# Graph network of four layers: the last two row chunks of layer 3 by gathered neighbour lists instead of dense products

## The chip, the cores and the metric

The kernel runs on one core of a Trainium2 chip. Times are device microseconds (us) of one execution. Three timed runs of the kernel before gave 2332.58, 2321.81 and 2318.35 us, so the median is 2321.81 us. The profile and the trace come from another execution, under the profiler, which took 2299.72 us; its span, from the first instruction to the last, is 2297.7 us.

The engines are called PE (TensorE, matrix products), PEld (its weight loads), DVE (VectorE), ACT (ScalarE), POOL (GpSimd) and SP (SyncE). A transfer (DMA) is issued by SP, ACT or POOL and carried by 16 DMA engines.

## The reference

A graph of 2708 nodes has a 0/1 adjacency matrix `adj` (about 0.6% ones, symmetric) and 512 features a node. Four layers follow each other, each with a residual and a layer norm:

```python
x = layernorm(x + relu((D(A + I)D x + x) W0 + b0))     # layer 0
x = layernorm(x + (D' A D' x) W1.T + b1)               # layer 1
x = layernorm(x + gat(gat(x)))                         # layer 2: two attention layers
#   gat(x): Wh, Ws = split(x W2); a = softmax(Wh Ws.T) * A; leaky_relu(a Wh + x)
x = layernorm(x + A x W3 + b3)                         # layer 3 (8 heads side by side: one 512x512 W3)
```

All of it is float32; the change is about layer 3, `A x W3`.

## The kernel before

**Tiles.** The nodes are cut into 22 blocks of 128 (`NB`; the last has 20 nodes). Output nodes are also cut into six chunks `CH`: chunks 0 to 3 have 512 nodes (four blocks each), chunk 4 has 384 (blocks 16 to 18), chunk 5 has 276 (blocks 19 to 21). The blocks that are summed over are cut into six groups `GROUPS`: four of four blocks, then two of three.

**Dense products (layers 0, 1 and 3).** `multiply` (line 894) forms the transposed sum `acc[d] = sum over j of x[j][:, d].T @ m[j]` for the four quarters `d` of the features, where `m[j]` is the 128 x 512 piece of the adjacency matrix. `prepare` (808) has ACT cast `m` from a byte mask, which SP loads (`load_bytes`, 798), one group ahead of the products. x is held as a high and a low part, so a (chunk, block) pair costs eight products[...]. `evict` (969) copies `acc` to `ht`, and `project` (986) multiplies by the weights in float32[...]: 16 products for a chunk of four blocks. `residual` (1015) fetches the rows `xres` of x for the skip connection, `biased` (1021) adds the bias to them on DVE, `combine` (1027) adds the projection, and `finish` (1058) normalizes and stores.

**Attention (layer 2).** After softmax, scores times neighbours are not formed densely. For each node block, layer 1 made lists of the nodes that have a neighbour in the block (`index`, 1200, into `givers`): four lists of 128 for the whole block and two for each quarter of it, twelve in all; the block of 20 has three. Attention writes a table `pairs` to DRAM, whose row for a node holds the node's features next to its weights. `fetch` (1677) has POOL gather the 128 rows of a list into one of eleven buffers `g`, and `weigh` (1732) multiplies weights by features on PE, in float32. While this goes on, `early` (605) already runs layer 3's products for chunks 0, 1 and 2 (`TWO = 3`) over the first 16 blocks, and puts the sums aside as `begun`. `Attention.normalize` (1796) ends a chunk of the last attention layer and stores its rows as `saved[2]`, from where layer 3 reads its residuals.

**Order.** Each engine works through its instructions in the order in which the code issues them (`Ordered`, 54). SP and POOL issue transfers in that order too, and a wait at one holds all behind it. Eight completion semaphores serve the transfers of SP; a transfer first waits for the one eight before it. PSUM has two halves of four banks. A chunk's four `acc`, its four projections and the next chunk's `acc` in the same half take the same four banks in turn: the next `acc` waits until DVE's `combine` has read the projection before it.

**The last stage.** After attention, layer 3 does groups 4 and 5 of chunks 0 and 1, then of chunk 2, then chunks 3, 4 and 5 whole. The projection of a chunk comes one step after its products (`step`, 1120, and `ends`, 1180).

Of the kernel before, what the change touches and what calls it, by code (L numbers as in the profile page):

```python
# [19 lines left out]
P = 128  # L20
N = 2708
# [20 lines left out]
FAR = 4096  # L42
PAGES, WIDES = 82, 11
TWO = 3
LN_EPS = 1e-5
DEG_EPS = 1e-8
SLOPE = 0.01
# [40 lines left out]
class Kernel:  # L88


    def __init__(self, ctx, tc, x_in, x_t, adj, adj_t, w0, b0, w1, b1, w2, w2_t, w3, b3, out):
        self.tc, self.nc = tc, tc.nc
        nc = self.nc
        self.ctx = ctx
        self.x_in, self.x_t, self.adj, self.adj_t, self.out = x_in, x_t, adj, adj_t, out
        self.w0, self.b0, self.w1, self.b1, self.w2 = w0, b0, w1, b1, w2
        self.w2_t, self.w3, self.b3 = w2_t, w3, b3
        const = ctx.enter_context(tc.tile_pool(name="const", bufs=1))
        self.small = ctx.enter_context(tc.tile_pool(name="small", bufs=4))
        scratch = ctx.enter_context(tc.tile_pool(name="scratch", bufs=1, space=DRAM))  # L100
        tile_ = lambda name, shape, dt: const.tile(shape, dt, tag=name, name=name)
        self.ident = tile_("ident", [P, P], FP)
        self.ones = tile_("ones", [P, P], FP)
        self.ones_b = tile_("ones_b", [P, P], BF)

        self.rdeg = tile_("rdeg", [P, NB], FP)
        self.dis = tile_("dis", [P, NB], FP)
        self.nbad = len(CH) * NB
        self.bad = tile_("bad", [P, self.nbad + NB], FP)


        self.feeds = tile_("feeds", [P, NB, QUARTERS, NB], BF)
        self.givers = tile_("givers", [P, NB, LISTS], I32)

        self.base = tile_("base", [P, QUARTERS], FP)
        self.upto = tile_("upto", [P, P], BF)
        self.node = tile_("node", [P, 1], FP)
        self.block = tile_("block", [P, NB], BF)
        self.since = tile_("since", [P, P], BF)
        self.saved = [  # L120
            [scratch.tile([P, D], FP, tag=f"x{s}_{i}", name=f"x{s}_{i}") for i in range(NB)]
            for s in range(3)
        ]
        self.between = [
            scratch.tile([P, D], FP, tag=f"y_{i}", name=f"y_{i}") for i in range(NB)
        ]

        self.masks = [
            scratch.tile([P, NB, w], U8, tag=f"mask{k}", name=f"mask{k}")
            for k, (_, w) in enumerate(CH)  # L130
        ]

        self.turned = [
            [
                scratch.tile([P, DC, w], FP, tag=f"t{s}_{k}", name=f"t{s}_{k}")
                for k, (_, w) in enumerate(CH)
            ]
            for s in range(2)
        ]
# [345 lines left out]
    return rest + [[q * ONLY + t for q in range(QUARTERS)] for t in range(ONLY)]  # L485


def cost(columns):

    return 4 * columns / 2400  # L490
# [25 lines left out]
class Fast:  # L516
# [18 lines left out]
    def run(self):  # L535
        kernel, nc = self.k, self.nc
        with ExitStack() as ctx:
            pool = lambda name, bufs, **kw: ctx.enter_context(
                self.tc.tile_pool(name=name, bufs=bufs, reuse_waits="tile", **kw)
            )  # L540
            self.pages, self.wides = pool("pages", PAGES), pool("wides", WIDES)
            self.small, self.lists = pool("small_f", 4), pool("lists", 1)
            self.banks = [pool(f"banks{h}", 4, space=PSUM) for h in range(2)]
            given = [kernel.x_in[bass.ts(i, P), :] for i in range(NB)]
            l0 = Layer(0, given, kernel.w0, kernel.b0)
            l1 = Layer(1, kernel.saved[0], kernel.w1, kernel.b1)
            l3 = Layer(3, kernel.saved[2], kernel.w3, kernel.b3)
            self.attention = attention = Attention(self)
            self.jobs, self.due, self.other, self.beats = [], None, 1, 0
            run = Run(l0, l1)  # L550
            for t in range(len(run.seq)):
                self.step(run, t)
            attention.project(attention.layers[0], 0)
            for g in range(3):
                self.ends(run, g)
                if g == 1:
                    attention.project(attention.layers[0], 1)


            run = Run(l3)  # L560
            run.seq = [(l3, k, g) for k in range(TWO) for g in range(4)]
            run.seq += [(l3, k, g) for g in (4, 5) for k in range(2)]
            run.seq += [(l3, k, g) for k in range(2, TWO) for g in (4, 5)]
            run.seq += [(l3, k, g) for k in range(TWO, len(CH)) for g in range(len(GROUPS))]
            attention.run(self.early(run))
            for j in range(*GROUPS[5]):
                l3.rows[j] = attention.made[j]
            for t in range(4 * TWO, len(run.seq)):
                self.step(run, t)

            ly, k = run.before
            parts = self.project(ly, k)
            for some in (parts[:-1], parts[-1:]):
                made = []
                for i, n, ps in some:
                    made.append((i, n, self.combine(ly, k, len(made), i, n, ps)))
                self.finish(ly, k, made)
# [230 lines left out]
    def prepare(self, ly, k, g, between=None, late=False):  # L808


        nc, (c0, cw) = self.nc, CH[k]
        ats = ly.done.pop(("at", k, g), None)
        if ats is None:
            return
        ms = []
        for j, at in zip(range(*GROUPS[g]), ats):
            if k == 0:
                self.halve(ly, j)
            m = self.page(f"m{ly.number}_{k}_{j}", FR)
            nc.scalar.copy(m[:, :cw], at[:, :cw])  # L820
            ms.append(m)
            if between:
                between()
                between = None
        ly.done["m", k, g] = ms
        if ly.number == 0:
            self.examining = self.examine(ly, k, g, ats)
            if k == 0 or g > 0:
                self.checked()
            else:  # L830
                next(self.examining)
        if ly.number == 1:
            at = ly.done.pop(("bytes", k, g))
            if late:
                return lambda: self.note(k, g, at)
            self.note(k, g, at)

    def note(self, k, g, at):

# [54 lines left out]
    def multiply(self, ly, k, g, only=None, ds=range(DC)):  # L894
# [3 lines left out]
        starts, stops = ((0, 16), (15, NB - 2)) if two else ((0,), (NB - 2,))  # L898
        if blocks[0] in starts and 0 in ds:

            half = 0 if two and blocks[0] == 0 else k
            ly.acc[k] = [self.bank(half, f"acc{ly.number}_{k}_{d}") for d in range(DC)]
        ms = ly.done["m", k, g]
        if blocks[-1] == NB - 1:
# [16 lines left out]
        for d, j in todo:  # L921
            for x, first in ((ly.hi, True), (ly.lo, False)):
                nc.tensor.matmul(
                    ly.acc[k][d][:, :cw],
                    x[j][:, bass.ts(d, P)],
                    ms[j - GROUPS[g][0]][:, :cw],
                    start=(j in starts and first),
                    stop=(j in stops and not first),
                )

    def degrees(self, ly, k):
        nc, cw = self.nc, CH[k][1]
# [53 lines left out]
    def project(self, ly, k):  # L986
# [4 lines left out]
        for i, lo, n in sorted(blocks_of(k), key=lambda b: b[2] > QW):  # L991
            if n <= QW:
                ps = self.few(
                    k,
                    f"mm{ly.number}_{i}",
                    n,
                    D,
# [2 lines left out]
                )  # L1000
                parts.append((i, n, ps))
                continue
            ps = self.bank(k, f"mm{ly.number}_{i}")
            for c in range(DC):
                nc.tensor.matmul(
                    ps[:n],
# [8 lines left out]
    def residual(self, ly, k):  # L1015
        for i, _, _ in blocks_of(k):
            t = self.page(f"xres{ly.number}_{i}")
            self.nc.gpsimd.dma_start(t, ly.source[i])
            ly.done["xres", i] = t

    def biased(self, ly, k):
# [98 lines left out]
    def step(self, run, t):  # L1120
# [5 lines left out]
            self.attention.blank()  # L1126
        if ly.number == 1 and k == len(CH) - 1 and g in (2, 3, 4):
            self.attention.begin(g - 2)
        if ly.number == 0 and g == len(GROUPS) - 1:
            self.multiply(ly, k, g, ds=range(2))  # L1130
            ends = self.degree_ends(ly, k)
            next(ends)
            self.multiply(ly, k, g, ds=range(2, DC))
        else:
            self.multiply(ly, k, g)
        if g == len(GROUPS) - 1 and k in ly.begun:
            self.evict(ly, k)
        wide = CH[k][1] == BANK
# [1 line left out]
            self.work("PE")  # L1140
        if run.before:
            self.ends(run, run.phase)
            run.phase += 1
            if run.phase in ((3, 4, 5) if wide else (4,)):
                self.work("DVE")
# [239 lines left out]
class Attention:  # L1385
# [29 lines left out]
    def blank(self):  # L1415
# [3 lines left out]
        for pairs in (p for ly in self.pairs for p in ly):  # L1419
            self.nc.sync.dma_start(  # L1420
                pairs[N:, : 2 * PAIR + D].rearrange("j (r d) -> j r d", d=D),
                t[:n, :].unsqueeze(1).to_broadcast([n, (2 * PAIR + D) // D, D]),
            )

    def begin(self, step):

# [369 lines left out]
    def normalize(self, ch):  # L1796
# [4 lines left out]
        def rest():  # L1801
            for _ in work:
                pass
            for (i, _, _), (r, _) in zip(ch.blocks, ch.ends):
                self.nc.sync.dma_start(self.k.saved[2][i], r)
                self.made[i] = r

        self.later(4, rest)


    def run(self, next_layer):
# [108 lines left out]
            yield from self.project_steps(ly, k)  # L1920


@with_exitstack
def kernel(
    ctx: ExitStack,
# [60 lines left out]
```

## Time and profile before

| What | Value |
|---|---|
| Median of the timed runs | 2321.81 us (2318.35 to 2332.58) |
| The profiled execution, its span | 2299.72 us, 2297.7 us |
| PE busy | 2269.4 us, 99% of the span |
| DVE, ACT, POOL busy | 1391.5, 675.5, 705.4 us |
| Moved by DMA | 486.34 MB, 212 GB/s on average |
| Attention's last list product on PE | starts at 2087.05 us |
| Last layer 3 product over the mask | ends at about 2277 us |

A window line of the profile gives, for a stretch of the span, each engine's busy time with its count of instructions, then the granted PE clock (1.00 is full speed), the share of the DMA engines that was busy, and GB/s. A line of the chain gives start, duration, and the engine, line and tile of the work that set the end. Almost all instructions go through a helper that keeps the order, so they carry its line, L71, and are told apart by their tiles. Each float32 product stands in the records as two.

### The profile page before, as it was taken

What the parts mean: (1) busy time and instruction counts of PE and PEld (TensorE: products, weight loads), DVE (VectorE), ACT (ScalarE), POOL (GpSimd) and SP (SyncE); (2) the same over time, 40 slices, a digit from 0 to 9 for tenths busy, and PEclk for the clock granted to TensorE, in tenths of its full rate; (3) what the DMA queues carried; (4) which work ended last, traced back from release to release, by engine and by line L of the source; (5) the groups of instructions that cost most, each with busy time, mean ns of one, the idle gap of its engine ahead of it and who ended that gap; (6) DMA issues with size and microseconds to landing.
All of it is one profiled execution on the core that took longest, in us unless ns stands there. A gap on an engine that the chain in (4) does not pass through costs nothing.

```text
span 2297.7 us, 25903 instructions
## 1 busy us (share of the span) xinstructions
PE 2269.4 (99%) x8525; PEld 1289.0 (56%) x8525; DVE 1391.5 (61%) x2803; ACT 675.5 (29%) x1354; POOL 705.4 (31%) x822
## 2 busy tenths in 40 slices
PE   9999999999999999999999999999999999899997
PEld 6776876777644444443555444444443555466685
DVE  6777787786553537748667511238769788525523
ACT  7444452322111123223322200113223334342211
POOL 3433431111000001635557540001635467442000
PEclk9999999999999999999999999999999999999999
DMA  9966752223547415858789997405868799963311
GB/s 351 286 188 184 199 168 81 76 81 104 208 184 267 144 25 184 303 191 297 254 311 360 349 412 284 183 8 179 303 218 286 254 322 339 334 217 120 116 51 43
DMA packets 260929, 486.34 MB, mean 212 GB/s; under 512 B 40238, under 2 KB 126950, under 8 KB 260784
## 3 DMA queue, kind: packets, MB, share of 16 engines
q1 hardware_dynamic: 192128, 269.63, 33.6%
q0 software_dynamic: 68656, 214.96, 28.0%
q8 instruction: 69, 1.13, 0.2%
q14 instruction: 76, 0.62, 0.1%
HBM read 307.55 MB, written 176.92 MB: 211 GB/s over the span
## 4 chain that ended last, share of the span: by engine, by line
PE 86%; DMA 6%; DVE 4%; ACT 1%; issue 1%; POOL 1%; SPq 0%; ACTq 0%; POOLq 0%; DVEq 0%
PE sp L71 33%; PE acc L71 30%; PE mm L71 8%; PE z L71 6%; PE wst L71 6%; DMA x<-x 2%; DMA x<-in_x 1%; DMA at<-in_adj_t 1%; DMA g<-pairs,givers 1%; PE mix L71 1%; DMA pairs<-s 1%; POOL xt L71 1%; PE list L71 1%; ACT m L71 1%; PE tr_x2t L71 0%
## 5 line engine op out<-in xcount | busy, mean ns | idle before, releaser
L71 PE MATMUL sp<-xs,wst_sb 128*128 128x512 f32 (+3 forms) x2112 | 798.3, 544 | 0.0
L71 POOL DMA_INDIRECT g<-pairs,givers x510 | 524.2, 1028 | 872.9 <-issue 338.9
L71 PEld LDWEIGHTS sp<-xs,wst_sb 128*128 128x128 f32 (+1 forms) x2112 | 379.7, 186 | 408.4 <-issue 324.8
L71 PE MATMUL acc<-m,xh 128*128 128x512 f32 (+4 forms) x1584 | 566.8, 379 | 6.6 <-ACT m L71 5.1
L71 PE MATMUL acc<-m,xl 128*128 128x512 f32 (+4 forms) x1584 | 549.6, 365 | 2.0 <-DVE xl L71 1.8
L71 PEld LDWEIGHTS acc<-m,xh 128*128 128x128 f32 (+1 forms) x1584 | 288.0, 188 | 70.9 <-issue 21.3
L71 PEld LDWEIGHTS acc<-m,xl 128*128 128x128 f32 (+1 forms) x1584 | 288.3, 188 | 46.3 <-issue 5.3
L71 PE MATMUL acc<-g 128*32 128x512 f32 (+1 forms) x1020 | 264.8, 606 | 4.6 <-DMA g<-pairs,givers 4.0
L71 ACT COPY s<-sp 128x512 f32<-128x512 f32 (+2 forms) x252 | 132.7, 528 | 396.8 <-PE sp L71 395.1
L71 ACT ACTIVATE s<-s 128x512 f32<-128x512 f32 (+3 forms) x264 | 151.6, 580 | 319.8 <-DVE s L71 319.5
L71 DVE TENSOR_TENSOR top<-top,s 128x512 f32<-128x512 f32 (+2 forms) x240 | 149.1, 621 | 156.1 <-ACT s L71 154.5
L71 PE MATMUL mm<-w,ht 128*128 128x512 f32 (+1 forms) x528 | 223.7, 593 | 0.0
L71 ACT CAST m<-at 128x512 fp32r<-128x512 uint8 (+5 forms) x396 | 199.2, 567 | 62.3 <-DMA at<-mask 19.7
L71 DVE TENSOR_TENSOR s<-s,shift 128x512 f32<-128x512 f32 (+3 forms) x264 | 162.7, 620 | 36.2 <-ACT shift L71 36.2
L71 DVE TENSOR_TENSOR s<-s,a 128x512 f32<-128x512 f32 (+3 forms) x264 | 165.8, 628 | 13.6 <-DMA a<-mask 4.5
L71 DVE TENSOR_TENSOR sum<-sum,s 128x512 f32<-128x512 f32 (+4 forms) x252 | 156.5, 621 | 15.4 <-ACT s L71 15.4
L71 PEld LDWEIGHTS mm<-w,ht 128*128 128x128 f32 (+1 forms) x528 | 95.8, 186 | 117.0 <-issue 112.2
L71 PEld LDWEIGHTS acc<-g 128*32 128x32 f32 (+1 forms) x1020 | 74.6, 134 | 148.0 <-issue 116.5
L71 PE MATMUL z<-w,xt 128*128 128x512 f32 (+1 forms) x352 | 151.0, 596 | 0.0
L71 PE MATMUL wst<-xt,mixed 128*128 128x512 f32 (+2 forms) x384 | 150.5, 544 | 0.0
L71 POOL DMA_DIRECT2D x<-o x44 | 26.0, 597 | 329.7 <-DVE o L71 325.4
L71 PEld LDWEIGHTS wst<-xt,mixed 128*128 128x128 f32 x384 | 72.0, 190 | 71.1 <-issue 58.8
(168 smaller groups left out, 1476.7 us busy)
## 6 DMA issues: line engine op xcount, KB each, us to landing
pairs<-z_sb SPq DMA_DIRECT2D x84, 768.0 KB
pairs<-s SPq DMA_DIRECT2D x168, 256.0 KB
at<-in_adj_t SPq DMA_DIRECT2D x84, 256.0 KB
xres<-x POOLq DMA_DIRECT2D x44, 256.0 KB, 4.6
x<-o POOLq DMA_DIRECT2D x43, 256.0 KB, 3.4
pairs<-s SPq DMA_DIRECT2D x84, 128.0 KB
x<-x SPq DMA_DIRECT2D x37, 256.0 KB
at<-mask SPq DMA_DIRECT2D x32, 256.0 KB
```

Of the source, the lines that this page charges most:

```text
L71: ins = call(*args, **kw)
```

## The change

Chunks 4 and 5 of layer 3 (blocks 16 to 21) are computed as attention does it, from a table `sided` in DRAM. A row of it holds a node's adjacency weights and its features, three copies of the features with weights between them (2196 numbers a row).

1. The weights of chunks 4 and 5 are written in layer 1: after each cast of `m`, `give` has ACT issue two transfers of it to the table, 88 in all.
2. The features of blocks 0 to 11 are written by SP from `Attention.normalize`, three copies in one transfer (`aside`), twelve transfers of 768 KB.
3. The features of blocks 12 to 21 are written after attention, by SP, from `saved[2]`: ten transfers of 768 KB from DRAM to DRAM.
4. `Listed` then fetches 63 lists with POOL, multiplies, turns the sum with PE's transposes, projects, and ends the blocks in pairs. Its products are put between those of chunk 3.
5. Order of the last stage: groups 4 and 5 of chunks 0 and 1, chunk 3 whole with the lists beside it, then groups 4 and 5 of chunk 2. `half_of` gives the PSUM halves for that order.
6. `residual` of layer 3 issues its loads from SP instead of POOL.
7. `blank` writes zeros to the table's unused rows.

```diff
+DENSE = 4
+LISTED = CH[DENSE][0] // P
+SIDED = D + 2 * P
...
             run.seq += [(l3, k, g) for g in (4, 5) for k in range(2)]
+            run.seq += [(l3, k, g) for k in range(TWO, DENSE) for g in range(len(GROUPS))]
             run.seq += [(l3, k, g) for k in range(2, TWO) for g in (4, 5)]
-            run.seq += [(l3, k, g) for k in range(TWO, len(CH)) for g in range(len(GROUPS))]
             attention.run(self.early(run))
             for j in range(*GROUPS[5]):
                 l3.rows[j] = attention.made[j]
+            for i in range(CH[TWO][0] // P, NB):
+                attention.aside(i, kernel.saved[2][i])
+            self.listed = Listed(self, l3)
             for t in range(4 * TWO, len(run.seq)):
+                if t == len(run.seq) - 2:
+                    self.listed.end_all()
                 self.step(run, t)
...
             m = self.page(f"m{ly.number}_{k}_{j}", FR)
             nc.scalar.copy(m[:, :cw], at[:, :cw])
             ms.append(m)
+            if ly.number == 1 and k >= DENSE:
+                self.give(k, j, m)
...
+    def give(self, k, j, m):
+        n, lo, cw = rows_of(j), 0, CH[k][1]
+        while lo < cw:
+            i = (CH[k][0] + lo) // P - LISTED
+            w = min(P if i % 2 == 0 else 2 * P, cw - lo)
+            at = i // 2 * SIDED + i % 2 * (D + P)
+            self.nc.scalar.dma_start(
+                self.k.sided[j * P : j * P + n, at : at + w], m.bitcast(FP)[:n, lo : lo + w]
+            )
+            lo += w
...
+    def half_of(self, ly, k):
+        return k if ly.number < 3 else (0, 1, 1, 0)[k]
...
             t = self.page(f"xres{ly.number}_{i}")
-            self.nc.gpsimd.dma_start(t, ly.source[i])
+            (self.nc.sync if ly.number == 3 else self.nc.gpsimd).dma_start(t, ly.source[i])
...
                 self.nc.sync.dma_start(self.k.saved[2][i], r)
+                if ch.k < TWO:
+                    self.aside(i, r)
...
+    def aside(self, i, rows):
+        to, copies = self.k.sided[i * P : (i + 1) * P, P:], (NB - LISTED) // 2
+        self.nc.sync.dma_start(
+            bass.AP(to.tensor, to.offset, [to.ap[0], (SIDED, copies), (1, D)]),
+            rows.unsqueeze(1).to_broadcast([P, copies, D]),
+        )
...
+class Listed:
+    AHEAD = WIDES - 1
...
+    def fetch_ahead(self):
+        nc = self.nc
+        while self.to_fetch and len(self.fetched) < self.AHEAD:
+            i, t = self.to_fetch.pop(0)
+            if ("xres", i) not in self.ly.done:
+                x = self.ly.done["xres", i] = self.f.page(f"xres3_{i}")
+                nc.sync.dma_start(x, self.ly.source[i])
+            g = self.f.wide(f"g3_{i}_{t}")
...
+            nc.gpsimd.indirect_dma_start(
+                out=g[:, :width],
+                out_offset=None,
+                in_=self.k.sided[:, :],
+                in_offset=bass.IndirectOffsetOnAxis(ap=self.k.givers[:, i, t : t + 1], axis=0),
+                element_offset=(i - LISTED) // 2 * SIDED + first,
+            )
...
+    def weigh(self, wait=False):
...
+        for h, g in enumerate(gs):
+            lo, rows = (h * QW, QW) if side else (0, n)
+            e, z = (D + lo, 0) if odd else (0, P - lo)
+            nc.tensor.matmul(
+                self.acc[lo : lo + rows],
+                g[:, e : e + rows],
+                g[:, z : z + D],
+                start=first,
+                stop=last,
+            )
...
+    def turn(self, i, n, acc):
...
+        r = f.page(f"sum3_{i}")
+        nc.vector.tensor_copy(r[:n], acc[:n])
+
+        def turn():
+            ps = f.bank(self.half, f"tr3_{i}", (P, DC, P))
+            for c in range(DC):
+                nc.tensor.transpose(
+                    ps[:, c, :n], r[:n, bass.ts(c, P)], self.k.ident[:n, :n]
+                )
+            t = f.page(f"turned3_{i}", FP, (P, DC, P))
+            nc.scalar.copy(t[:, :, :n], ps[:, :, :n])
+            x = self.ly.done["xres", i]
+            nc.vector.tensor_add(x[:n], x[:n], self.ly.bt[:n])
+            self.advance(0.45)
+            self.later(2, lambda: self.project(i, n, t))
+
+        self.later(2, turn)
```

## The prediction

> **What bounds the kernel now.** I read the busy table first, then windows of the last 400 us, then the chain in order of time, then the timelines of PE, DVE, POOL and SP around the change.
>
> ```profile
> PE 2269.4 (99%) x8525; PEld 1289.0 (56%) x8525; DVE 1391.5 (61%) x2803; ACT 675.5 (29%) x1354; POOL 705.4 (31%) x822
> ...
> 1900.00:1950.00 50.00, 47.29 (x199) 28.34 (x198) 45.58 (x92) 20.21 (x46) 36.94 (x35) 1.00 1.01 357
> 1950.00:2000.00 50.00, 42.66 (x150) 22.29 (x148) 26.23 (x62) 17.75 (x33) 26.96 (x30) 0.95 0.94 351
> 2000.00:2090.00 90.00, 88.53 (x381) 59.15 (x380) 33.17 (x76) 32.27 (x64) 40.62 (x45) 0.99 0.68 216
> 2090.00:2276.00 186.00, 186.00 (x822) 134.75 (x821) 73.19 (x160) 42.98 (x100) 9.64 (x18) 1.00 0.22 75
> ```
>
> PE has no idle time in the last stage (186 of 186 us): there every product removed counts, and every wait added counts too. From 1900 to 2000 it is another matter: the DMA engines are full (1.01 and 0.94) and PE idles 10 us.
>
> ```profile
> 1921.51 11.97 DMA x<-x
> 1933.50 8.83 DMA pairs<-s
> ...
> 1956.06 10.54 DMA x<-x
> 1966.67 11.98 DMA x<-x
> ...
> 2110.89 13.73 PE mm L71 x32
> ...
> 2206.62 13.73 PE mm L71 x32
> 2220.35 28.38 PE acc L71 x175
> 2248.73 10.30 PE mm L71 x24
> 2259.03 18.06 PE acc L71 x143
> ```
>
> The chain shows the prices of the last stage, and that around 1920 to 1980 loads of 256 KB stand 10 to 12 us behind other transfers. Next, when the residual rows of chunk 0 are there and who needs them (POOL, SP, then DVE):
>
> ```profile
> 2080.07 2.24 POOL L71 DMA_DIRECT2D xres<-x  x4
> ...
> 2094.17 1.31 SPq L71 DMA_DIRECT2D x<-r  x3
> ...
> 2107.03 2.48 DVE L71 TENSOR_TENSOR xres<-xres,bias 128x512 f32<-128x512 f32 x4
> 2109.44 2.47 DVE L71 TENSOR_TENSOR ht<-acc,begun 128x512 f32<-128x512 f32 x4
> ```
>
> POOL asks for them at 2080, so DVE adds the bias at 2107 without waiting and goes on to chunk 1's `ht`. SP stores the last rows of attention at 2094.
>
> **What the Trainium skill says.** "DMA: Bandwidth & Descriptors", Latency and other measured facts: copies between two DRAM tensors run at 207 to 214 GB/s in each direction. The trace of before has no such copy; it has loads and stores mixed at 412 GB/s in its best slice, so a copy that both reads and writes DRAM at half of that fits. Same page, Issuing engines are not separate DMA queues: all issuers share 16 engines. The trace agrees, with loads 12 us late at share 1.01. Same page, Anatomy of one DMA: about 2 us fixed per transfer; quiet stores here land after 2.7 us at the least. "TensorE: Matmul & The Clock Gate", Part 1: after some 3.4 us of idleness PE runs at half rate for as long. The trace agrees: after an idle 4.08 us before 1997.27, four pairs of products take 1.04 us each instead of 0.45.
>
> **The change, part by part**, against the profiled execution (span 2297.7, execution 2299.72 us).
>
> *Products removed.* Of chunk 5, groups 1 to 5 are the last 18.06 us; its group 0 (32 products at 0.128) is 4.1. The 28.38 us piece is chunk 4's groups 1 to 5 and that 4.1, so 24.3; its group 0 (32 at 0.174) is 5.6. Together **-52.0**. Six projections remain: 18 us in either kernel.
>
> *Products added.* In attention's part of the chain a pair of whole lists takes 1.72 us and four quarter lists 0.99. A block is 2 x 1.72 + 2 x 0.99 = 5.4, five blocks 27.1, the block of 20 (three lists at 0.86) 2.6: **+29.7**. The turns: 24 transposes at 0.13 (10.9 us for 84) give **+2.7**. Net on PE: -19.6.
>
> *End of the lists.* For block 20 nothing covers DVE's copy of the sum (0.69) and ACT's copy of the turn (0.6), with handovers **+1.8**. The other blocks have a quarter chunk's products (1.8 us) and list products between. *Tail:* the last chunk has four blocks instead of three. Behind its `ht` DVE must finish chunk 3's last two blocks, its normalization, and four bias adds, before the first sum. I find the last DVE sum some 2.9 us after PE's last product; before it was 0.8. **+2.3**.
>
> *Fetches.* 63 at 1.26 us (0.95 and 0.30 between) are 79 us of POOL, beside 77 us of PE work from the first list to the last, with ten fetched ahead. If they start 11 us before the first list, they cost nothing; without that cover each us late is a us lost. They start when the table is whole, see below.
>
> *Writes of weights.* Each cast of `m` in layer 1's chunks 4 and 5 is followed on ACT by two issues that wait for it. The trace has no issue on ACT; SP's cost 0.32 to 0.46 us. So a block costs ACT 0.5 + 0.1 + 0.7 = 1.3 us, and PE needs 1.4 (chunk 4) or 1.0 us (chunk 5) for its products, with projections and turns between (562 to 596 us for chunk 5's 22 blocks, against 29 us of ACT and its own copies). Queued behind are the later casts, on which PE waits. Lower bound 0, upper 6 (22 x 0.3). I take **+2**: the last two groups come late.
>
> *Feature copies in attention.* Four of 768 KB a chunk are 3.1 MB, 8.6 us at 360 GB/s. Chunk 0's come at 1692 and chunk 1's at 1791; there POOL has just begun to fetch, and PE weighs only at 1714 and 1814, so I cost these at nothing (without that slack, up to 8 each). Chunk 2's come at 1888. Until 1900 about 4 us of DMA time are free, then none until 1985; on SP chunk 4's `pairs`, the masks and the x loads of layer 3 are behind them. **+5**, bounds 0 and 12.
>
> *Late copies and the residuals behind them.* This is the large term. SP issues the ten copies from 2095.5, 7.86 MB. At 214 GB/s that is 36.7 us, with 1.5 to start: over at 2133.7. In SP's queue the residual loads now come after them: two for the lists, then blocks 0 to 3. Block 3's is the sixth of 256 KB; 4.6 us at 340 GB/s and 2 to land give 2140.3. DVE meets `biased` for chunk 0 at 2107 and waits there. Behind it are chunk 1's `ht` and chunk 0's `combine`, and chunk 3's four `acc` need the banks that `combine` frees. PE would be through chunk 3's group 0 at 2090.7 + 20.2 (groups 4 and 5) + 13.7 (projection) + 7.3 = 2131.9. Now DVE ends the last bias add at 2140.9, `ht` at 2143.4, the first sum at 2144.1 (quarter d0 may start), the second at 2145.7, then statistics and four bias adds for chunk 1, the third sum at 2149.7, the fourth at 2151.3. PE leaves group 0 at 2153.1: 21.2 us late. The fetches start at about 2136 and share the engines with these loads, some 2 us more. **+23**. Bounds: at 390 GB/s (a store-like rate, 20 us) it is +4; at 150 GB/s (52 us) +38. As PE stands so long, the fetches get their ten ahead and cost nothing more.
>
> *Blank rows* are four small issues in layer 0, beside 250 GB/s of loads: 0.
>
> Sum: -19.6 + 1.8 + 2.3 + 2 + 5 + 23 = +14.5, so 2314.2 for the profiled execution's 2299.72. The median of the timed runs is 22 us (1.0%) higher than this execution; I scale: 2321.81 x 1.0063 = **2336 us**, +0.6%.
>
> **Rivals.**
> *Fast copies.* If DRAM to DRAM runs as stores do (340 GB/s, 23 us), the residual term is 23 - 13.6 = +9, the sum about 0: 2322. For it: 412 GB/s in a slice. Against it: every byte both leaves and enters DRAM.
> *The saving shows.* If the residuals do not wait for the copies (loads overtaking them in the rings), 23 falls to 0 and the sum is -8.5: 2313; with the attention and ACT terms at nothing too, 2306. Against it: 12 us behind other transfers in the chain above.
> *Slow copies, on the other side.* Pieces of 2 KB at 150 GB/s take 52 us. DVE gets past `biased` only at 2156, the term is +38 and the sum +30: 2352, slower by 1.3%. It becomes slower by over 1% when the copies need more than 46 us. For it: the copies go in pieces of 2 KB, three from the same row. Against it: stores of the same pieces ran at 390 GB/s between 1350 and 1400.
>
> **How the numbers follow.** A measurement of this kernel can tell about 1% from no change. Forecast (copies near 200 GB/s) 0.50, mostly between 2325 and 2346; fast copies 0.17; the saving shows 0.10; slow copies or a longer stall 0.23. Faster by over 1% (below 2298.6) needs more than all the PE time that is saved: 0.04. Slower by over 1% (above 2345): most of the slow case and the top of the forecast, 0.30. Within 1%: 0.66. The range leaves out the best of the saving and the worst of the slow case: 2308 to 2357.
>
> **What would show it.** PE idle in the last stage after chunk 0's projection, with DVE in `biased` waiting for `xres` until about 2140; `sided` copies on SP from 2095 and first fetches about 2136; then no waits on lists. More PE idle time than 10 us between 1900 and 2010. ACT's share higher in 500 to 600 us with PE short of `m` by 2 us. PE's busy time down by about 20 us. I am wrong if the copies are over by 2115, if DVE does not stand at the bias, or if PE waits on lists.

## The result and the profile after

The changed kernel takes 2352.98 us (median, 2344.19 to 2358.07); the kernel before, timed beside it, 2320.12 us. The ratio is 1.0122 with a 95% interval of 1.0089 to 1.0154: slower by 1.2%. On another chip, where the kernel before takes 2303.5 us, it is 1.0096 (1.0074 to 1.0119). The time lies in the range given, 17 us above the forecast. How it comes about is less well forecast than that suggests.

The first lines are the changed kernel's own page: engine shares, then the transfer queue of ACT, which is new.

```profile
PE 2279.2 (97%) x8323; PEld 1260.4 (53%) x8323; DVE 1393.7 (59%) x2812; ACT 662.1 (28%) x1313; POOL 753.5 (32%) x863
...
q10 hardware_dynamic: 12216, 7.15, 1.0%
```

PE has 202 products fewer, but its busy time is not lower (2279.2 us, before 2269.4) and its share falls from 99% to 97%: it stands idle more, and more of its products run at half clock (the mean granted clock is 0.984, before 0.997).

The first two traces are not a good pair. They lie 58.6 us apart, the timed runs 33 us: that trace of the kernel before was quicker by 20 us than its timed runs, and 10 us of the lag arise between 1165 and 1311 us, where nothing is changed. So both kernels were profiled again, on two chips where the kernel before takes 2304.25 and 2303.51 us (these executions took 2301.73 and 2326.64 us); below "before" and "after" are those two. Windows of after: layer 0's start, the end of layer 1, attention where the DMA engines are full, and the last stage (columns as in the prediction).

```profile
20.00:120.00 100.00, 97.75 (x407) 72.98 (x406) 69.85 (x170) 57.53 (x110) 35.76 (x57) 0.98 0.96 306
542.00:617.00 75.00, 65.23 (x419) 56.04 (x418) 43.03 (x97) 19.68 (x48) 11.63 (x21) 0.93 0.63 201
1906.00:2068.00 162.00, 147.73 (x585) 89.64 (x585) 105.43 (x229) 61.47 (x127) 93.20 (x90) 0.95 0.92 325
2116.20:2324.90 208.70, 181.29 (x646) 100.17 (x644) 85.25 (x199) 28.38 (x61) 60.92 (x63) 0.94 0.61 196
```

And of before, nearly the same work (it runs earlier there):

```profile
20.00:120.00 100.00, 98.90 (x419) 74.01 (x418) 72.09 (x177) 59.16 (x113) 36.75 (x57) 1.00 0.96 304
540.00:600.00 60.00, 60.00 (x410) 52.18 (x409) 41.20 (x94) 17.07 (x48) 11.67 (x21) 1.00 0.56 189
1890.00:2045.00 155.00, 144.44 (x583) 88.66 (x576) 105.77 (x229) 60.77 (x126) 89.99 (x88) 0.98 0.90 315
2093.50:2299.70 206.20, 194.06 (x847) 137.77 (x845) 82.58 (x190) 43.36 (x102) 9.67 (x18) 0.98 0.21 71
```

Layer 1's end, which had no gap, now has 9.8 us of them and a clock of 0.93; the last stage is 2.5 us longer although PE works 12.8 us less in it. Over the whole span PE's busy time falls by 4.8 us (2271.0 to 2266.2), where the forecast had about 20: products that run at half clock (granted clock 0.50) add 12.3 us more than in before. Following the same DVE instructions through both traces, after lags by:

| Stretch (us of before) | Lag added | Forecast |
|---|---|---|
| to 112 (layer 0) | +2.7 | 0 |
| 112 to 520 | +1.3 | 0 |
| 520 to 620 (end of layer 1) | +12.6 | +2 |
| 620 to 1741 | +0.3 | 0 |
| 1741 to 2042 (attention) | +5.9 | +5 |
| the rest | +2.4 | +7.5 |
| sum | +25.2 | +14.5 |

The last stage, step by step, in after: SP's queue, POOL's first fetch, DVE, then PE. Columns are start and duration in us, then engine, line, operation, tile (SPq and ACTq: SP or ACT issuing transfers); in brackets the idle time before and what the profile infers ended it. (That can be a neighbour: in the program POOL's first fetch waits for the copies.)

```profile
2120.08 16.83 SPq L76 DMA_DIRECT2D sided<-x  x10
2137.01 15.18 SPq L76 DMA_DIRECT2D xres<-x  x10
...
2151.57 0.96 POOL L76 DMA_INDIRECT g<-sided,givers  x1 [46.86 <-DMA xres<-x]
...
2152.57 2.55 DVE L76 TENSOR_TENSOR xres<-xres,bias 128x512 f32<-128x512 f32 x4 [20.84 <-DMA xres<-x]
2155.03 2.47 DVE L76 TENSOR_TENSOR ht<-acc,begun 128x512 f32<-128x512 f32 x4
...
2158.25 0.77 PE L76 MATMUL acc<-m,xh 128*128 128x512 f32 x1 [9.06 <-DVE xres L76]
```

This is the chain of the forecast, link by link: copies, residuals behind them, DVE idle at the bias 20.84 us, then chunk 1's `ht`, then `combine`, and PE 9.06 us without work before chunk 3's first products. What differs is the length: DVE starts the bias adds 32.5 us after the first copy was issued and ends them after about 35, where the forecast had it end them after 45.4.

### The profile page after: what moved, and what is told of

Its sections match the earlier page's. It is cut to its first block, busy times and chain, and to the rows that moved or that the text cites. A ratio compares the mean times of both kernels' runs of the same rounds, so it can differ in the third digit from the quotient of the medians.

```text
span 2356.3 us, 25725 instructions
## 1 busy us (share of the span) xinstructions
PE 2279.2 (97%) x8323; PEld 1260.4 (53%) x8323; DVE 1393.7 (59%) x2812; ACT 662.1 (28%) x1313; POOL 753.5 (32%) x863
## 4 chain that ended last, share of the span: by engine, by line
PE 77%; DVE 8%; DMA 5%; issue 4%; SPq 3%; ACT 2%; ACTq 0%; POOL 0%; another core or an unknown queue 0%; DVEq 0%
PE sp L76 29%; PE acc L76 26%; PE mm L76 8%; PE z L76 6%; PE wst L76 6%; SPq L76 3%; DVE s L76 2%; DVE sum L76 1%; ACT m L76 1%; PE mix L76 1%; DMA at<-in_adj_t 1%; DVE xres L76 1%; DVE top L76 1%; DMA x<-in_x 1%; DMA pairs<-s 1%
## 5 line engine op out<-in xcount | busy, mean ns | idle before, releaser
L76 PE MATMUL acc<-m,xh 128*128 128x512 f32 (+3 forms) x1408 | 527.0, 394 | 34.6 <-ACT m L76 22.7
L76 PE MATMUL acc<-m,xl 128*128 128x512 f32 (+3 forms) x1408 | 505.9, 376 | 1.8 <-DVE top L76 1.4
L76 PEld LDWEIGHTS acc<-m,xh 128*128 128x128 f32 (+1 forms) x1408 | 260.6, 191 | 105.5 <-issue 35.9
L76 PE MATMUL acc<-g 128*32 128x512 f32 (+2 forms) x1146 | 301.1, 607 | 5.7 <-DMA g<-pairs,givers 2.8
L76 PEld LDWEIGHTS acc<-m,xl 128*128 128x128 f32 (+1 forms) x1408 | 260.9, 192 | 49.4 <-issue 8.4
L76 ACT CAST m<-at 128x512 fp32r<-128x512 uint8 (+5 forms) x352 | 185.8, 578 | 102.0 <-ACT m L76 22.3
L76 PE MATMUL mm<-w,ht 128*128 128x512 f32 (+1 forms) x480 | 204.6, 593 | 0.0
L76 PEld LDWEIGHTS acc<-g 128*32 128x32 f32 (+2 forms) x1146 | 84.3, 135 | 168.2 <-issue 138.5
L76 PEld LDWEIGHTS mm<-w,ht 128*128 128x128 f32 (+1 forms) x480 | 88.1, 187 | 107.1 <-issue 102.7
```

Source lines behind the costliest of these rows:

```text
L76: ins = call(*args, **kw)
```

## Experiments

Some expectations below quote times of the first comparison; since chips differ, the ratio to the kernel before on the same chip is what can be compared. Experiments 1 to 4 ran on a chip where the kernel before takes 2304.25 us, 5 to 8 on one where it takes 2303.51, 9 on a slower one. The lag is always that behind the second trace of before.

Theory after the traces: three waits make up the loss. The residuals stand behind the copies (9 us of idle time and half clock after it); the writes of weights from cast tiles slow the end of layer 1 (12.6); chunk 2's feature copies meet full DMA engines (5.9). The rivals are in the expectations: other executions differ as much, the bytes are the cost whoever issues them, or the next wait takes each one's place.

**1. The kernel before again** (no edit).

> The kernel before, unchanged, profiled once more, to see how much of the lag between the two traces is only one execution differing from another. If the steps of lag that lie where the change touches nothing (about 10 us between 1165 and 1311 us, about 7 us near 93 us) are variation, this execution has them in part too and takes 2305 to 2332 us. If they belong to the change, its trace lies within 5 us of the first one all along and it takes about 2300 us. Between 540 and 600 us and in the last stage I expect PE without gaps, as in the first.

2301.73 us, within 4 us of the first trace everywhere and 2.0 us behind it at the end. By 112 us it is 2.2 us behind, over 1 us of that from the place near 95 us, where PE waits 1.1 us and waited 0.4 in the first trace: so that place varies by itself. Nothing is lost at 1165 to 1311 us, so by this run alone those 10 us seemed to belong to the change; experiments 5 and 9 show that they don't.

**2. Weight writes issued by SP.**

```diff
-            self.nc.scalar.dma_start(
+            self.nc.sync.dma_start(
                 self.k.sided[j * P : j * P + n, at : at + w], m.bitcast(FP)[:n, lo : lo + w]
```

> The changed kernel with the 88 weight writes of layer 1 issued by SP instead of ACT, nothing else. Theory (the issues cost ACT more than I put down, and the casts of m queue behind them): PE's idle time between 550 and 620 us, 10.8 us, and the 4.9 us of half clock after it go to under 3 together, and the time falls by 12 to 16 us from 2353, to 2337 to 2341. Rival one (the transfers themselves, their DMA time or their completion semaphores, are the cost, whoever issues them): no change, 2350 to 2355, with PE still waiting for m. Rival two (SP, waiting for each cast, holds up the mask loads behind it): PE or ACT waits for masks in layer 1 and the time is 2355 to 2365.

Ratio 1.0088 (1.0053 to 1.0122). The timed runs don't tell that from the changed kernel's 1.0096. The lag added from 520 to 620 us is 9.5 us, against 12.6 in after (13.7 to 15.7 in the other three traces with ACT's writes): a small part of the gain expected. What is left looks like the second rival. One gap remains, and SP's own waits between 540 and 612 us name its cause, the wait for casts, behind which the last mask load comes late (it is issued at 596.77 and lands at 605.4, together with an earlier write that the cast also waits for):

```profile
606.59 0.60 PE L76 MATMUL acc<-m,xh 32*128 32x276 f32 x4 [7.55 <-ACT m L76]
```

```profile
SPq L76 <- ACT m L76: 26.2, 9, 10.7
```

(A line of the waits: who waited for what, us in total, times, the longest.)

**3. Residuals of chunks 0 and 1 ahead of the copies.**

```diff
+            for k in range(2):
+                self.residual(l3, k)
             for i in range(CH[TWO][0] // P, NB):
                 attention.aside(i, kernel.saved[2][i])
...
-            self.residual(ly, k)
+            if not (ly.number == 3 and k < 2):
+                self.residual(ly, k)
```

> The changed kernel with the residual loads of layer 3's chunks 0 and 1 issued on SP ahead of the ten DRAM to DRAM copies, nothing else. Theory (DVE stands at the bias because the residuals are behind the copies): DVE's idle 21.6 us before the bias add and PE's idle 9.8 us before chunk 3's first products go, with about 2.3 us of half clock; the time falls by 9 to 12 us, to 2341 to 2344. Rival (the fetches, which still start only when the copies are over, become what PE waits for): PE idles 5 to 10 us at acc from g between 2175 and 2190, and the time falls by 0 to 5 us, to 2348 to 2353. If the copies need PE's stall for nothing, both traces show the copies over at the same time, some 27 us after their first issue.

Ratio 1.0087 (1.0059 to 1.0115), by itself not to be told from 1.0096. The trace is clear: DVE adds the bias at 2134.62 without waiting, while the copies are still running:

```profile
2123.16 4.41 SPq L76 DMA_DIRECT2D xres<-x  x8
2127.62 16.33 SPq L76 DMA_DIRECT2D sided<-x  x10
...
2158.67 0.96 POOL L76 DMA_INDIRECT g<-sided,givers  x1 [50.93 <-DMA out<-o]
...
2134.62 2.49 DVE L76 TENSOR_TENSOR xres<-xres,bias 128x512 f32<-128x512 f32 x4
```

PE's gap before chunk 3 is gone, and the last stage ends 9.6 us earlier against before than it began (after: 2.4 later). PE takes the first list at 2174.97, 16 us after its fetch was issued, so no wait for lists takes the place of the one removed. The theory holds in the last stage, which is 12 us shorter against before than that of after, as expected; from the first copy to the first fetch 31.0 us pass, in after 31.5, so the copies don't gain from PE's standing still.

**4. Both edits.**

> Both edits together: weight writes on SP, residuals of chunks 0 and 1 ahead of the copies. If both theories hold the gains add, 21 to 28 us from 2353: 2325 to 2332, level with the kernel before within 0.5%. If only the first holds 2337 to 2341, if only the second 2341 to 2344, if neither 2350 to 2355. What then remains against the kernel before is the time lost at the ends of the lists in the last stage (about 15 us of idle time and half clock) and some 5 us in attention.

Ratio 1.0033 (1.0023 to 1.0044). On the same chip each edit alone gives 1.0088 and 1.0087, with intervals that don't reach this one: so either edit gains about 0.0055 where the other is present. Against after, on another chip, give_sp wins 0.0008 and res_first 0.0009 by their middles, the two together 0.0063; each single one is uncertain by 0.003, so that they only add is neither shown nor excluded. In the traces they do add: 9.3 us between 520 and 620 us, and a last stage without the first gap.

**5. The changed kernel again** (no edit).

> The changed kernel, unchanged, profiled once more on this chip. Its ratio to the kernel before should be 1.009 to 1.015 as in the first comparison. Theory (the two gaps of PE near 2245 and 2282 us in its first trace, 2.5 and 2.3 us with half clock after them, and the 10 us between 1165 and 1311 us, belong to that one execution): they are gone, and the last stage costs 0 to 4 us more than that of the kernel before instead of 14. Rival (they belong to the turns of the lists' sums, and the two other edits removed them by chance): they are there again.

The ratio is given above. The two gaps near 2245 and 2282 us and the 10 us at 1165 to 1311 us are gone; the last stage costs 2.4 us. The theory holds, but "one execution" was too narrow: gaps in the last stage and those 10 us return on another chip (experiment 9, and the last section).

**6. Weights copied from the adjacency matrix in DRAM**, on top of 3. The transposed matrix that the kernel is given holds the same numbers; no cast tile and no engine is waited for, and the four zero stores of the table are not needed.

```diff
-            if ly.number == 1 and k >= DENSE:
-                self.give(k, j, m)
...
+        if ly.number == 1 and k in (1, 2, 3):
+            for part in ((0, 3), (1,), (2,))[k - 1]:
+                self.give(part, g)
...
+        self.nc.sync.dma_start(
+            self.k.sided[rows, at : at + w], self.k.adj_t[rows, c0 : c0 + w]
+        )
```

> Residuals ahead of the copies, and the weights of the table not written from the cast tiles at all: SP copies them from the transposed adjacency matrix in DRAM to the table, 24 transfers of up to 512 KB in layer 1's chunks 1 to 3, which wait for no engine; they cover the unused rows, so the four extra writes of zeros go too. Theory (SP's mask loads stood behind the writes of ACT, because a transfer waits for the one eight before it, and the four writes of zeros held SP's loads in layer 0): PE has no gap between 550 and 620 us and at most 1.5 us near 95 us, the lag on the kernel before is under 3 us at 620 us, where it was 13 to 24, and the ratio falls from 1.0033 to 0.996 to 0.999. Rival (the bytes themselves are the cost): PE waits for masks or lists in layer 1 and the ratio stays at 1.002 to 1.005.

Ratio 0.9983 (0.9971 to 0.9995). The end of layer 1 is as in the kernel before:

```profile
550.00:620.00 70.00, 70.00 (x448) 55.87 (x447) 46.75 (x98) 17.36 (x48) 11.64 (x21) 1.00 0.48 162
```

The same 7 MB cost nothing here, so the bytes are not the cost; how they are issued is: here 24 large transfers from SP, earlier in the layer, that wait for no cast, instead of 88 small ones between casts. Which of these differences counts for how much, this run can't tell. One part of the expectation fell: near 95 us this kernel loses 8.0 us, where at most 1.5 were expected, without any zero store to the table. Those four stores are not the cause of that loss.

**7. Chunk 2's features late too**, on top of 6.

```diff
-                if ch.k < TWO:
+                if ch.k < TWO - 1:
                     self.aside(i, r)
...
-            for i in range(CH[TWO][0] // P, NB):
+            for i in range(CH[TWO - 1][0] // P, NB):
```

> As from_input, with the four feature copies of chunk 2 issued after attention too (fourteen copies there instead of ten) and not at 1888 us, where the DMA engines are full. Theory (those four cost about 5 us in attention, and the last copies have some 13 us to spare before PE asks for the first list): the lag grows by under 2 us between 1900 and 2050 us, the copies take about 37 us instead of 27, PE still never waits for a list, and the ratio is 0.001 to 0.002 below that of from_input. Rival (attention's own loads set those gaps, and the later fetches now come late): no gain between 1900 and 2050 us, PE waits for lists by 2 to 8 us, the ratio is level or up to 0.003 above.

Ratio 0.9978 (0.9968 to 0.9989), which the interval doesn't tell from that of 6. The traces do: between 1741 and 2042 us the lag changes by -0.8 us, in from_input by +8.6. (It grows by 2.5 to 8.6 us in the five traces with chunk 2's copies there on these two chips, and by -0.8 and, in experiment 8, -2.1 in the two without.) The first fetch comes 42.0 us after the first copy is issued instead of 31.0, and PE waits for lists 0.9 us in all: not never, as the theory had it, but less than the rival's 2 to 8. The window of from_input, then that of this kernel:

```profile
1905.00:2060.00 155.00, 140.35 (x538) 82.90 (x538) 97.66 (x212) 57.59 (x120) 86.99 (x85) 0.94 0.90 322
1905.00:2060.00 155.00, 143.88 (x581) 88.94 (x580) 99.89 (x220) 65.53 (x134) 90.37 (x89) 0.99 0.90 317
```

The 3.15 MB of the four further copies after attention take 11.0 us: 286 GB/s.

**8. Chunk 3's bias adds earlier in DVE's order**, on top of 7.

```diff
+        if self.listed and (k, g) == (DENSE - 1, len(GROUPS) - 1):
+            self.biased(ly, k)
...
-            if ly.number == 3:
+            if ly.number == 3 and k != DENSE - 1:
                 self.biased(ly, k)
```

> As chunk2_late, with the four bias adds of chunk 3 put ahead of that chunk's last products in DVE's order. Theory (at the end of the lists DVE does four bias adds and two copies of sums before the sum of block 20, on which PE waits 2.8 us and then runs at half clock): PE's gap before the transposes of block 20 shrinks to under 1 us, and the ratio falls by 0.001 to 0.002. Rival (DVE only waits for PE's last product there): the gap stays at 2.8 us.

Ratio 0.9966 (0.9942 to 0.9991). In after DVE did this while PE waited for `sum`:

```profile
2261.66 2.46 DVE L76 TENSOR_TENSOR xres<-xres,bias 128x512 f32<-128x512 f32 x4
2264.05 1.28 DVE L76 COPY ht<-acc 128x512 f32<-128x512 f32 x2
2265.24 0.68 DVE L76 COPY sum<-acc 128x512 f32<-128x512 f32 x1
...
2265.98 0.65 PE L76 MATMUL tr<-ident,sum 128*128 128x128 f32 x4 [2.78 <-DVE sum L76]
2267.31 5.11 PE L76 MATMUL mm<-w,turned 128*128 128x512 f32 x8 [0.68 <-ACT turned L76]
```

In bias_first the wait for the sum is 0.9 us, and no half clock follows:

```profile
PE tr L76 <- DVE sum L76: 0.9, 1, 0.9
```

The theory holds for the gap. In time it can't be seen: the interval holds the ratio of 7 too. By its middle this is the lowest ratio of all versions.

**9. Four runs on a slower chip**, where the kernel before takes 2326.34 us. First, mask loads of layer 1's chunks 4 and 5 on POOL:

```diff
-        self.nc.sync.dma_start(at[:, : j1 - j0, :], self.k.masks[k][:, j0:j1, :])
+        queue = self.nc.gpsimd if ly.number == 1 and k >= DENSE else self.nc.sync
+        queue.dma_start(at[:, : j1 - j0, :], self.k.masks[k][:, j0:j1, :])
```

> The changed kernel with layer 1's mask loads of chunks 4 and 5 issued by POOL instead of SP; ACT still writes the weights. Theory (the writes of ACT hurt mainly because SP's mask loads wait for the completion of earlier transfers, which are those of ACT): with the loads on POOL, which shares no completion semaphores with ACT here, PE's lost time between 550 and 620 us (12 to 16 us of gaps and half clock) falls to under 5 us, all of it waiting for casts. Rival (the issues cost ACT itself the time): the gaps stay at 8 to 15 us. Time about 2312 to 2318 us against 2326 if the theory holds.

2350.55 us in one execution; the time expected was meant for the chip of experiment 5, so only the trace answers. 10.5 us of gaps and 3.4 of half clock remain near 550 to 625 us. The theory as put falls: the mask loads in SP's queue are not what costs most. ACT's waits there show what is left:

```profile
ACT m L76 <- ACT m L76: 12.5, 14, 1.0
...
ACT m L76 <- DMA sided<-m: 10.7, 4, 7.9
```

ACT spends its own time on the issues, and then stands at a write that has not finished. The same stands in after: SP waits 42.4 us for ACT's writes between 540 and 612 us, and the pair of writes that ACT issues at 600.63 takes 4.56 us instead of 0.9; the cast behind it is released when a weight load of SP lands, and PE waits for that cast:

```profile
SPq L76 <- DMA sided<-m: 42.4, 9, 12.1
```

```profile
600.63 4.56 ACTq L76 DMA_DIRECT2D sided<-m  x2
605.23 0.42 ACT L76 CAST m<-at 128x276 fp32r<-128x276 uint8 x1 [4.63 <-DMA w<-in_w]
605.70 0.60 PE L76 MATMUL acc<-m,xh 128*128 128x276 f32 x1 [4.53 <-ACT m L76]
```

So the two queues hold each other up. The trace's records of the issues name the completion semaphores: SP's and ACT's transfers take numbers 100 to 107 in turn, POOL's take 111 to 118. The second write of that pair takes number 103, which SP's weight load of 598.07 still holds; the load lands at 604.84, and ACT issues the write at 604.86. This wait alone makes 4.53 of the 9.8 us of gaps. How the rest of the 12.6 us divides between such waits and ACT's time for the issues stays open; the loads that are waited for also take 6.8 to 8.3 us each to land there, and no run tested why.

Then two runs on the loss near 95 us. The table declared in the kernel before, and one small store to it:

```diff
+        self.sided = scratch.tile([NP, 2196], FP, tag="sided", name="sided")
...
+        if ly.number == 1 and (k, g) == (1, 0):
+            self.nc.sync.dma_start(self.k.sided[:P, :P], self.k.ones)
```

> The kernel before with the table of 2816 x 2196 numbers declared in DRAM at the same place as in the changed kernel, and one 64 KB store to it in layer 1; nothing else. All eight traces of kernels with the table lose 2.6 to 8.0 us near 95 us, with or without writes of zeros, and the two traces of the kernel before lose nothing there. Theory (where the other buffers then lie in DRAM sets how fast layer 0's loads come): 2 to 8 us are lost near 95 us here too and the time is 2304 to 2310 us. Rival (something that the changed kernels issue): under 1.5 us are lost near 95 us, the time is 2300 to 2303 us.

2.6 us are lost near 95 us, as the theory has it, but on another chip than the second trace of before; one trace doesn't settle it. The time, 2323.04 us, can't be set against the one expected, which was for a quicker chip. Between 1165 and 1311 us this kernel loses 6 us against before, and the other three traces of this chip 9 to 10, one of them again without the change; the eight traces of the two quicker chips lose at most 0.9 there. So that loss goes with the chip and not with the change. And the zero stores to `pairs`, which both kernels have, moved:

```diff
-        if ly.number == 0 and (k, g) == (1, 0):
+        if ly.number == 1 and (k, g) == (1, 0):
             self.attention.blank()
```

> The kernel before with its four stores of zeros to the unused rows of pairs (3.5 MB) moved from layer 0's second chunk to layer 1's second chunk. Theory (these stores compete with layer 0's loads near 75 to 95 us): without the table there is at most 1.1 us to gain, so the ratio is 0.9990 to 1.0005; it serves as the measure for the next run.

> As bias_first, with the same stores of zeros moved to layer 1. Theory (the loss near 95 us comes from these stores in front of SP's loads, slower with the table in DRAM): the 4 to 8 us near 95 us go, and the ratio falls from 0.9966 to 0.994 to 0.996. Rival (the loads themselves are slower, whatever stands before them): the loss stays at 3 us or more and the ratio at 0.996 to 0.998.

The ratios are 0.9968 (0.9943 to 0.9993) and 0.9992 (0.9974 to 1.001). The first is lower than its expectation allowed (0.9990). Its trace gains 5.1 us on that of before_pad near 95 us, most of the 7 that the ratio gives; but before_pad has the table, and no trace of before itself was taken on this chip. The second missed the 0.994 to 0.996 expected. In both traces PE has no gap near 95 us and both are 2.5 us ahead of before after it (0.3 us ahead of its first trace). The loss is that of these stores, standing in SP's queue ahead of loads that ACT and PE wait for; how large it is varies between traces, from 0.4 us of gap in the first trace of before to 8.0 us in from_input. On this chip the version with all edits is level with the kernel before and not faster than the kernel before with this one edit.

## Why the prediction was right or wrong

**Right: what the stage is made of.** PE's busy time less what the half clock adds falls by 17.3 us in the last stage (forecast 19.6); the tail after PE's last product grows by 2.75 us (2.3); PE never waits for a list (0). The chain copies, residuals, bias, `ht`, `combine`, `acc` is the forecast's, and res_first shows that it is the cause of PE's wait.

**Wrong in size: "Late copies and the residuals behind them", +23.** It cost 9.06 us of idle time and 2.8 of half clock, 11.9. The term that failed most is the copy rate of 214 GB/s, taken from the Trainium skill ("DMA: Bandwidth & Descriptors", Latency and other measured facts). The page measures it on tiles of 128 partitions by 16 KiB and gives from 97 to 214 GB/s by row pitch; the prediction left that condition out. These copies go in pieces of 2 KB, and four more of them take 11.0 us (42.0 instead of 31.0 to the first fetch), 286 GB/s; the measurement decides. While only the copies run, after shows the same:

```profile
2124.00:2140.00 16.00, 16.00 (x70) 10.41 (x69) 2.77 (x4) 4.04 (x7) 0.00 (x0) 1.00 1.06 289
```

The prediction's second support, half of the 412 GB/s of before's best slice, is 206 and fails with it. The ten copies are over at most 30.6 us after the first was issued (POOL's wait for the last ends at 2150.65), where the forecast had 38.2 (36.7 and 1.5 to start): 7.6 of the 11.1 us between forecast and measurement. The rest lies behind them. The residual loads were given 4.6 us after the copies and 2 to land (taken from Anatomy of one DMA, a section about transfers that POOL issues); SP issued the last load that chunk 0 needs at 2146.68, before the copies were over, and DVE started 1.9 us after them. The 2 us for fetches that share the engines don't show. The rate lies between the forecast's and that of the fast rival, 340. (The bound of +4 at 390 GB/s is mis-added: the prediction's own steps give about 6.)

**Wrong: "Writes of weights", +2 with bounds 0 and 6.** It cost 12.6 us, outside its bounds. The step counted ACT's time per block nearly rightly, 1.3 us (where nothing is waited for, casts in after come every 1.30 us in chunk 5 and every 1.46 in chunk 4), but took a queue as a delay on its own engine only. It left out that transfers of ACT and SP wait on the same eight completion semaphores: the prediction knew the eight as SP's and did not ask who else now shares them. The largest gap, 4.53 us, is such a wait (experiment 9); for the rest the share of it is not shown.

**Wrong in size: "End of the lists", +1.8.** 2.78 and 0.68 us of idle time and 1.7 of half clock, 5.2. The step had DVE free at that point; chunk 3's bias adds and two copies to `ht`, 3.7 us, were queued ahead. bias_first shows it: with the bias adds moved, the two waits are 0.9 and 0.7 us, close to the forecast. The half clock came after 2.78 us of idle time, less than the 3.4 us that the prediction cites; the measurement decides, and none followed the 0.9 us in bias_first.

**Right: attention, +5.** 5.9 us, from chunk 2's copies: without them there is no loss (experiments 7 and 8). Chunk 1's delay DVE by 4.1 us at 1841 us and that is given back by 1900, so they cost nothing, as forecast.

**Not forecast: layer 0, 2.7 us.** The forecast put the table's four zero stores at nothing, and from_input, which leaves them out and loses more, doesn't speak against it. The loss comes with stores that were there before; why they cost more in every kernel with the table is open.

**The sum.** It is made on the second pair of traces, which come from two chips of nearly equal speed. With the measured terms (the last 1.3, between 112 and 520 us, has no cause found), -17.3 + 11.9 + 5.2 + 2.75 + 12.6 + 5.9 + 2.7 + 1.3 gives +25.1 us; the lag at the end is 25.2. In the last stage the terms must add up, as busy time, idle time and tail make up the stage. The 33 us between the timed runs of the first comparison are not accounted for in this way: their traces lie 58.6 us apart. Two misses of opposite sign, -11 for the copies and +10.6 for the weights, hid each other; that is luck, and what the total misses (+14.5 against +25.1) comes from the smaller terms. The time of the slow rival, 2352, was met while its mechanism, copies at 150 GB/s, was the reverse of what happened. The likeliest class, within 1%, was missed in the first comparison by 0.2% and met in the second by 0.04%, both within their intervals.

## What to carry to other kernels

When an engine starts to issue transfers, list whose completion semaphores they share: here ACT's write, and the cast behind it, waited 4 us for a weight load in SP's queue. A term that comes from a bandwidth of another shape deserves its whole range in the forecast: 214 GB/s became 286. Where the same bytes already lie in DRAM in the needed form, a copy from there waits for no engine, and its place in the program is free: the 12.6 us at the end of layer 1 went to nothing.

## What the runs showed that was not expected

The DRAM to DRAM copies in pieces of 2 KB, one read row written three times, moved 286 GB/s.

Chips differ by up to 23 us for the same kernel before (2303.5 to 2326.3 us), by the traces of before_pad and before_blank most of it in attention between 1165 and 1311 us and from 1650 to 2000 us. In its first trace and on the slower chip the changed kernel also loses more in its last stage. In blank_late, on that chip, ACT copies a turn 7 us after PE's transposes stand in the trace as done (the releaser it gives, "remote", names no engine):

```profile
2176.49 0.42 PE L76 MATMUL tr<-ident,sum 20*128 20x20 f32 x4
...
2184.13 0.23 ACT L76 COPY turned<-tr 128x80 f32<-128x80 f32 x1 [14.17 <-remote]
...
2184.41 1.92 PE L76 MATMUL mm<-w,turned 128*20 128x512 f32 x8 [2.88 <-ACT turned L76]
```

Three gaps of PE of 2.7 to 4.7 us lie in its last stage (this one, one behind DVE and one for which the profile names no cause), none in that of before_pad on the same chip, whose last stage has no lists. That PE's signals come late where list products run would fit the slower attention of both kernels, but no run tested it.
